# Attention by half batches, a first run fixed to expert 0, independent scatters and three transpose banks in an attention and mixture-of-experts kernel

## The chip, the cores and the metric

The kernel runs on one core of one Trainium2 chip. The metric is the device time of one execution in microseconds; the median of the runs is what counts. Beside it there is a profile of one execution, which shows every engine's instructions in time. The engines are TensorE (PE; its weight loads are shown as PEld), VectorE (DVE), ScalarE (ACT), GpSimd (POOL) and SyncE (SP, which here only issues DMAs). Each engine works through its own queue in order; an instruction that waits holds up everything behind it on that engine.

## What is computed

The inputs are x (4 x 1024 x 1024), a context (4 x 1024 x 256), the weights of a key projection and of eight experts, all float32.

```
kv   = ctx @ W_k.T + b_k
p    = layernorm(x)
out  = p @ kv                              # 1024 x 256 for each batch
sim  = (out @ kv.T) / 32
attn = softmax(layernorm(sim) * ln_gamma + ln_beta)
x1   = x + attn

h      = layernorm(x1)                      # 4096 tokens
probs  = softmax(h @ gate_w); the best two experts of each token, weights normed
y(tok) = sum over its two experts e of weight * ((silu(h @ w1[e]) * (h @ w3[e])) @ w2[e])
result = x1 + y
```

## The kernel before

The program has two stages, one after the other.

**Attention and routing.** Work is cut into 4 batches of 8 blocks of 128 tokens (G is 8, HG is 4 blocks, a half batch). `front(b)` is a list of 13 steps that a batch needs before its blocks can be finished: `context` (load and transpose the context), `values` (kv, and its bias on DVE), `keys` (transposed kv, centred), and for each of two halves four times `first_norm` (load a block of x, normalize it into `pn`, transpose it into `pT`) and once `attend` (32 matmuls' records into `pm_o`, copied to `oT`). `back(b, g)` finishes one block: four matmuls into `sim` (L323), the sum of squares on ACT (L330), a power on POOL (L198 and L200), `z` on DVE (L332), the row minimum (L334), the exponential on ACT (L338), `x1` on DVE (L342), its layernorm to `hn` (L206 to L210), the transposes of `hn` on PE (L217) with copies on ACT, the gate matmuls `pm_g` (L351) and a copy of the logits, `lg` (L360). `sim`, `z`, `x1`, `hn`, `pn` and the transposes each have two buffers. `route` takes the logits of several blocks, picks experts, and computes the slot of each token; `put` scatters the token ids to `id_d` (L450) from POOL.

The order of emission is: all of `front(0)`, then for each batch its eight `back` blocks, with the 13 steps of `front(b + 1)` spread between them; batch 3 has none to spread. A scheduler then sets the order on each engine, starting from this emission. After the last `route`, DVE computes a small table: the number of runs (`run_n`, L544), and for each run its expert, its kind and its first slot (`run_e`, `run_k`, `run_s`, L546 to L567).

**Experts.** Before the loop `load_rows` loads the ids of the first run's tokens (L686), clamps them on DVE (`rd`, L694), and gathers five groups of rows of h with POOL's indirect DMAs (L697). `load_first` loads the first tiles of w1 and w3. Both take the expert and the slot from the table through registers of SP. `tokens_in` transposes the rows: ten groups of four transposes into `pt_h` (L737), each copied by ACT or DVE (L742, L746), all through one bank of PSUM (the pool `pst`, one buffer).

The loop runs `run_n` times, eight in the profiled execution. Each run handles up to two token blocks of one expert, and all its PE work is in an order written by hand, with matmuls L838 for w1 and w3, and L894 for w2. At the end of a token block `tokens_out` transposes the output (`pt_y`, L783), adds it with the token's weight to the rows (L785), and scatters the rows to the result by an indirect DMA on POOL (L790). The last quarter of a run's last block is left for the next run, and after the loop for `leftover`, with the same bank and the same scatters. Scatters all write the result, and each waits for the one before.

Of the kernel before, what the change touches and what calls it, by code (L numbers as in the profile page):

```python
# [9 lines left out]
F32 = mybir.dt.float32  # L10
I32 = mybir.dt.int32
AF = mybir.ActivationFunctionType
ALU = mybir.AluOpType
# [6 lines left out]
P = 128  # L20
N = 512
# [4 lines left out]
MOST = HOLD[-1]  # L26
# [3 lines left out]
TOP_K = 2  # L30
# [4 lines left out]
def kernel(  # L35
# [14 lines left out]
    nc = tc.nc  # L50
# [8 lines left out]
    NT = T // P  # L59
    KM = M // P  # L60
    MAXQ = -(-T // MOST)
    NRUN = (T * TOP_K + E * (MOST - 1)) // MOST
    TAB = 16
    REG = T + -(-(MOST + P) // P) * P
    NONE = 2 * T
# [34 lines left out]
    with ExitStack() as st:  # L100
# [39 lines left out]
        def clear_slots():  # L140
            for r in range(0, E * REG, ID_R):
                n = min(ID_R, E * REG - r)
                step = nc.sync.dma_start(
                    out=id_d[r : r + n, :].rearrange("(p r) w -> p (r w)", p=P),
                    in_=none[:, : n // P * IDW],
                )
                tc.keep_in_program_order(step)
                cleared.append(step)
# [321 lines left out]
        base = None  # L470
        puts, to_put = [], []
        ready = []
        for i, step in enumerate(front(0)):
            step()
            if i == 3:
                later_loads()
        for b in range(B):
            todo = list(front(b + 1)) if b + 1 < B else []
            n_steps = len(todo)
            for g in range(G):  # L480
                back(b, g)
                for _ in range(min(len(to_put), TOP_K)):
                    to_put.pop(0)()
                while todo and (n_steps - len(todo)) * G < n_steps * (g + 1):
                    todo.pop(0)()
                if b == 0 and g == 0:
                    clear_slots()
                t = b * G + g
                if ready and t >= ready[0][1]:
                    u = ready.pop(0)[0]  # L490
                    base = route(u, lgs.pop(u), base)
                for u, (t0, m) in enumerate(GROUPS):
                    if t == t0 + m - 1:
                        ready.append((u, t + (1 if u >= len(GROUPS) - 3 else RG // 2)))
        for u, _ in ready:
            base = route(u, lgs.pop(u), base)
        for step in to_put:
# [5 lines left out]
        def row(name, n=E):  # L503
            return tb.tile([1, n], F32, name=name)
# [17 lines left out]
        for j in range(MAXQ):  # L522
            nc.vector.scalar_tensor_tensor(
                nr, n_e, float(j * MOST), nr, ALU.is_gt, ALU.add
            )
        kind, hold = row("kind"), row("hold")
        nc.vector.memset(kind, 0.0)
        nc.vector.memset(hold, float(HOLD[0]))
# [47 lines left out]
    with ExitStack() as st:  # L576
# [97 lines left out]
        def expert(i):  # L674
            return nc.values_load(
                run_e[:, ds(i, 1)], engines=(ENG.SP,), min_val=0, max_val=E - 1
            )

        def first_slot(i):
            return nc.values_load(  # L680
                run_s[:, ds(i, 1)], engines=(ENG.SP,), min_val=0, max_val=(E - 1) * REG + T
            )
# [11 lines left out]
            nc.vector.tensor_scalar(rd, ids[:, :, 0], T - 1, None, ALU.min)  # L694

        def gather(dst, src, rd, s, n):
            nc.gpsimd.indirect_dma_start(  # L697
                out=dst,
                out_offset=None,
                in_=src,  # L700
                in_offset=bass.IndirectOffsetOnAxis(ap=rd[:n, s : s + 1], axis=0),
            )
# [17 lines left out]
        def load_rows(s0):  # L720
            load_ids(ids0, s0)
            where_from(rd0, ids0)
            for s, r in enumerate(ROWS):
                gather(rows[s][:r, :], h_d, rd0, s, r)

        def load_first(i, j):

            weights(wts_in[j], (w1f, w3f)[j], expert(i), 0, KD, 0)

        def tokens_in(then=None):  # L730


            def step(s, h):
                r = ROWS[s]
                pt = pst.tile([P, 4, P], F32, tag="pt", name="pt_h")
                for k in range(HK):
                    nc.tensor.transpose(  # L737
                        pt[:, k, :r], rows[s][:r, ts(HK * h + k, P)], ident[:r, :r]
                    )
                dst = x[:, ds(HK * h, HK), ds(s * P, r)]  # L740
                if h % 2:
                    nc.vector.tensor_copy(dst, pt[:, :, :r])  # L742
                    if then is not None:
                        then(s)
                else:
                    nc.scalar.copy(dst, pt[:, :, :r])  # L746

            return [lambda s=s, h=h: step(s, h) for s in range(RT) for h in range(2)]
# [24 lines left out]
                p5=v[:, T1, :], p6=t2, p7=t[:, 1, :],  # L773
            )

        def tokens_out(ids, split, q, y):

            yv = y.rearrange("p (d c) -> p d c", d=2)

            def step(s, r):  # L780
                pt = pst.tile([P, 4, P], F32, tag="pt", name="pt_y")
                for d in range(2):
                    nc.tensor.transpose(pt[:r, d, :], yv[:, d, ds(s * P, r)], ident)  # L783
                part = rows[s][:r, ts(q, QW)]
                nc.vector.scalar_tensor_tensor(  # L785
                    part, pt[:r, 0:2, :].rearrange("p a b -> p (a b)"),
                    ids.bitcast(F32)[:r, s, 1:2], part, ALU.mult, ALU.add,
                )
                if q == DQ - 1:
                    nc.gpsimd.indirect_dma_start(  # L790
                        out=of,
                        out_offset=bass.IndirectOffsetOnAxis(ap=ids[:r, s, 0:1], axis=0),
                        in_=rows[s][:r, :],
                        in_offset=None,
                        bounds_check=T - 1,
                        oob_is_err=False,
                    )

            return [lambda s=s, r=r: step(s, r) for s, r in enumerate(split)]

        def leftover():
            return tokens_out(ids1, ROWS, DQ - 1, y1)

        def run(i, ex, s0, blocks, width):
            n = width // 2
# [10 lines left out]
            def take_ids():  # L816
# [3 lines left out]
                nc.vector.tensor_copy(rd, rd0)  # L820
                return ids, rd

            late = leftover()
            right = token_factors(n)
            for b in range(blocks):
# [41 lines left out]

                def rows_of_out(s):
                    if s < len(split):
                        gather(rows[s][: split[s], :], of, rd, s, split[s])  # L870

                late += tokens_in(rows_of_out)
                if not last:
# [1 line left out]
                for q in range(DQ):  # L875
                    pp = banks()
                    i2 = 0
                    for u, kn in enumerate(W2K):
                        j = load(w2f, 2 * i2, kn, q * QW)
                        left = weight_sums(j, kn, True)  # L880
                        todo = [
                            (p, k) for k in range(kn // 2) for p in ORDER
                        ] if u < len(W2K) - 1 else [
                            (p, k) for p in ORDER for k in range(kn // 2)
                        ]
                        if last and q == DQ - 1 and u == len(W2K) - 1:

                            assert j % WR == WR - 1 == 2
                            load_first(i + 1, 0)
                            load_first(i + 1, 1)  # L890
                            late.append(lambda: weight_sums(0, KD, False))
                        hid = [hidden_factors(g[:, i2 + k, :, :], n) for k in range(kn // 2)]
                        for at_m, (p, k) in enumerate(todo):
                            nc.tensor.matmul(  # L894
                                pp[p][:, :n], left[p][:, k, :], hid[k][p],
                                start=(i2 + k == 0), stop=(i2 + k == NI - 1),
                            )
                            if late and at_m % 7 == 6 and i2 + at_m // 7 > 0:
                                late.pop(0)()
                        i2 += kn // 2  # L900
                    if last and q == DQ - 1:
                        combine(pp, n, y1, XW)
                        break
                    y = gp.tile([P, 2 * XW], F32, tag="y", name="y", bufs=1)
                    combine(pp, n, y, XW)
                    late += tokens_out(ids, split, q, y)
            assert not late

        load_rows(first_slot(0))
        load_first(0, 0)  # L910
        load_first(0, 1)
        for step in tokens_in():
            step()
        weight_sums(0, KD, False)
        n_run = nc.values_load(run_n, min_val=1, max_val=NRUN)
        with tc.For_i(0, n_run) as i:  # L916
# [3 lines left out]
            for k in tc.Switch(kind, len(RUNS)):  # L920
                with tc.manual_schedule(engines={ENG.PE}):
                    run(i, ex, s0, *RUNS[k])
        for step in leftover():
            step()


# [26 lines left out]
```

## Time and profile before

| | before |
|---|---|
| median of 3 runs | 8942.93 us (8942.44 to 8948.6) |
| the profiled execution | 8943.72 us, span 8941.9 us |
| PE busy | 8736.7 us, 98% of the span |
| DVE busy | 4822.9 us, 54% |
| ACT busy | 666.7 us, 7% |
| POOL busy | 446.1 us, 5% |
| first loop matmul starts | 545.94 us |
| loop, to the last matmul's result | about 546 to 8918 us |

The span is the time from the first to the last instruction in the profile; the execution's own time lies 1.8 us above it. Busy times are sums over the whole span. The granted clock is the share of TensorE's full clock that it was given in a stretch. Rows of the timeline begin with the start and the duration in microseconds, then engine, line, operation, and tiles; in brackets stands the idle time of the engine before it, and what ended it. A row with a count (x8) is several instructions of the kind merged. A float32 matmul of the program shows as two records.

### The profile page before, as it was taken

To read this page: it belongs to the slowest core of one execution; us is meant where nothing else is said; L and a number is where in the kernel's file an instruction comes from. 1 tells how busy PE (TensorE), PEld (TensorE's weight loads), DVE (VectorE), ACT (ScalarE), POOL (GpSimd) and SP (SyncE) were. 2 spreads that over 40 slices of the span, in tenths; PEclk is the share of its full clock that TensorE was granted. 3 is DMA by queue.
4 is the path that set the end of the run, shared out by engine and by line. 5 is a ranking of instruction groups with operands and counts; after the bars stand their busy time and mean duration, and the time that the engine had idled before them with its cause. 6 is when DMAs were issued, how large, how long until landed. Compare 5 with 4: busy or idle time off the path is not lost. (4 is left out here: it accounts for less than half of the span.)

```text
span 8941.9 us, 99381 instructions
## 1 busy us (share of the span) xinstructions
PE 8736.7 (98%) x40738; PEld 7530.9 (84%) x40739; DVE 4822.9 (54%) x8820; ACT 666.7 (7%) x1170; POOL 446.1 (5%) x512
## 2 busy tenths in 40 slices
PE   8979999999999999999999999999999999999999
PEld 5569998999988888888888888888888888888887
DVE  5654645555554545546455554556555464555545
ACT  3310000000000000000000000000000000000000
POOL 2310000000000000000000000000000000000000
PEclk9979999999999999999999999999999999999999
DMA  3232332323232232323333232233323233232322
GB/s 140 110 101 88 105 105 91 110 93 112 96 104 83 91 103 89 103 91 102 101 95 101 92 108 84 95 103 94 110 93 103 86 103 96 90 102 91 105 87 93
DMA packets 769237, 882.16 MB, mean 99 GB/s; under 512 B 33424, under 2 KB 729232, under 8 KB 768608
## 3 DMA queue, kind: packets, MB, share of 16 engines
q1 hardware_dynamic: 734096, 766.12, 26.5%
q0 software_dynamic: 34368, 107.84, 3.6%
q8 instruction: 357, 5.85, 0.3%
q14 instruction: 272, 2.23, 0.1%
q10 hardware_dynamic: 144, 0.13, 0.0%
HBM read 803.61 MB, written 74.87 MB: 98 GB/s over the span
## 5 line engine op out<-in xcount | busy, mean ns | idle before, releaser
L838 PE MATMUL ps<-x,w 128*128 128x262 f32 (+5 forms) x10752 | 2489.2, 381 | 78.9 <-issue 77.8
L838 PEld LDWEIGHTS ps<-x,w 128*128 128x128 f32 x10752 | 2043.9, 191 | 370.3 <-issue 80.6
L838 PE MATMUL ps<-xs,s 128*128 128x262 f32 (+5 forms) x7168 | 1625.9, 379 | 0.0
L838 PEld LDWEIGHTS ps<-xs,s 128*128 128x128 f32 x7168 | 1355.0, 189 | 195.1
L633 DVE TENSOR_TENSOR s<-w 128x512 f32<-128x512 f32 (+2 forms) x769 | 479.6, 624 | 1638.1 <-DMA w<-in_L_ffn_w_dram 1634.4
L894 PE MATMUL ps<-g,s 128*128 128x262 f32 (+5 forms) x3584 | 1026.1, 379 | 0.0
L894 PE MATMUL ps<-t,w 128*128 128x262 f32 (+5 forms) x3584 | 1024.9, 379 | 0.0
L894 PE MATMUL ps<-g,w 128*128 128x262 f32 (+5 forms) x3584 | 904.6, 381 | 0.0
L838 PE MATMUL ps<-xs,w 128*128 128x262 f32 (+5 forms) x3584 | 848.2, 379 | 0.0
L838 PE MATMUL ps<-x,s 128*128 128x262 f32 (+5 forms) x3584 | 848.2, 380 | 0.0
L672 DVE TENSOR_TENSOR c<-ps,vu 128x524 f32<-128x524 f32 (+5 forms) x448 | 309.8, 691 | 919.7 <-PE ps L838 919.7
L894 PEld LDWEIGHTS ps<-g,s 128*128 128x128 f32 x3584 | 680.1, 190 | 95.3 <-DVE y L672 0.4
L838 PEld LDWEIGHTS ps<-x,s 128*128 128x128 f32 x3584 | 680.9, 190 | 94.1
L838 PEld LDWEIGHTS ps<-xs,w 128*128 128x128 f32 x3584 | 678.6, 189 | 96.4
L894 PEld LDWEIGHTS ps<-t,w 128*128 128x128 f32 x3584 | 678.8, 189 | 96.1
L766 DVE TENSOR_TENSOR t<-g 128x262 f32<-128x262 f32 (+5 forms) x896 | 375.5, 424 | 677.1 <-PE ps L894 674.0
L894 PEld LDWEIGHTS ps<-g,w 128*128 128x128 f32 x3584 | 651.4, 190 | 76.6
L767 DVE TENSOR_TENSOR t<-g,t 128x524 f32<-128x524 f32 (+5 forms) x896 | 613.1, 689 | 16.5
L663 ACT COPY p1s<-ps 128x262 f32<-128x262 f32 (+5 forms) x512 | 191.1, 373 | 4623.5 <-PE ps L838 2432.9
L894 PE MATMUL ps<-t,s 128*128 128x262 f32 (+5 forms) x1792 | 512.9, 380 | 0.0
L634 DVE TENSOR_TENSOR s<-s,w 128x512 f32<-128x512 f32 (+2 forms) x769 | 475.9, 619 | 10.1
L635 DVE TENSOR_TENSOR s<-w,s 128x512 f32<-128x512 f32 (+2 forms) x769 | 474.4, 617 | 0.0
(170 smaller groups left out, 4863.8 us busy)
## 6 DMA issues: line engine op xcount, KB each, us to landing
w<-in_L_ffn_w_dram SPq DMA_DIRECT2D x450, 1024.0 KB, 5.1
w<-in_L_ffn_w_dram SPq DMA_DIRECT2D x256, 768.0 KB, 4.5
w<-in_L_ffn_w_dram SPq DMA_DIRECT2D x64, 512.0 KB, 3.5
xt<-in_x_dram SPq DMA_DIRECT2D x32, 512.0 KB, 4.3
out_dram<-x SPq DMA_DIRECT2D x32, 512.0 KB, 2.9
h_d<-hn SPq DMA_DIRECT2D x32, 512.0 KB, 2.6
cx<-in_ctx_dram SPq DMA_DIRECT2D x4, 1024.0 KB, 5.5
id_d<-none SPq DMA_DIRECT2D x5, 512.0 KB, 10.7
```

The lines of the kernel that those rows point to most:

```text
L633: nc.vector.tensor_tensor(f["p5"], a21, a22, ALU.add)
L634: nc.vector.tensor_tensor(f["p6"], f["p5"], a11, ALU.subtract)
L635: nc.vector.tensor_tensor(f["p3"], a12, f["p6"], ALU.subtract)
L663: nc.scalar.copy(p1s, one[:, :n])
L672: nc.vector.tensor_tensor(mid, qc[:, :, :n], vu, ALU.add)
L766: nc.vector.tensor_tensor(t2, v[:, B22, :], v[:, T1, :], ALU.subtract)
L767: nc.vector.tensor_tensor(t[:, 1:3, :], v[:, B11 : B21 + 1 : B21 - B11, :], t2.unsqueeze(1).to_broadcast([P, 2, n]), ALU.subtract,)
L838: nc.tensor.matmul(pp[p][:, :n], left[p][:, k, :], right[p][:, k, :], start=(k == 0), stop=(k == HK - 1),)
L894: nc.tensor.matmul(pp[p][:, :n], left[p][:, k, :], hid[k][p], start=(i2 + k == 0), stop=(i2 + k == NI - 1),)
```

## The change

The list of `front` steps of each batch is cut in two: `context` (of the next batch) goes to the half before, then `values`, `keys`, four norms and the first attend are a half, and four norms and the second attend are another. Only the first half of batch 0 is emitted ahead of the blocks. Then, for each four blocks, the steps of the next half are spread between them. So the last four blocks of all have no steps between them, where before it was the last eight.

Expert 0 is given one run at least (`nr` of expert 0 is at least 1), so that the first run is always expert 0's and its first slot is 0: the loads before the loop use constants. The number of runs that the table may hold is computed to match (it is 15 either way).

The scatters of one token block are declared independent of each other. The gathers of result rows are made to wait for the scatters that were sent since the run began. Outside the loop the transposes use the three double banks of the matmuls (`ps2`), not the single one.

```diff
-    NRUN = (T * TOP_K + E * (MOST - 1)) // MOST
+    NRUN = (T * TOP_K + E * MOST - (E - 1)) // MOST
...
-        for i, step in enumerate(front(0)):
+        halves = []
+        for b in range(B):
+            steps = list(front(b))
+            cut = 3 + HG + 1
+            halves.append(steps[1:cut])
+            halves.append(steps[cut:])
+            if b == 0:
+                first_steps = [steps[0]] + halves.pop(0)
+            else:
+                halves[-3].append(steps[0])
+        for i, step in enumerate(first_steps):
             step()
             if i == 3:
                 later_loads()
-        for b in range(B):
-            todo = list(front(b + 1)) if b + 1 < B else []
-            n_steps = len(todo)
-            for g in range(G):
-                back(b, g)
...
-                while todo and (n_steps - len(todo)) * G < n_steps * (g + 1):
-                    todo.pop(0)()
...
+        for t in range(NT):
+            if t % HG == 0:
+                todo = halves.pop(0) if halves else []
+                n_steps = len(todo)
+            back(*divmod(t, G))
+            for _ in range(min(len(to_put), TOP_K)):
+                to_put.pop(0)()
+            while todo and (n_steps - len(todo)) * HG < n_steps * (t % HG + 1):
+                todo.pop(0)()
...
+        nc.vector.tensor_scalar(nr[:, 0:1], nr[:, 0:1], 1.0, None, ALU.max)
...
         def gather(dst, src, rd, s, n):
-            nc.gpsimd.indirect_dma_start(
+            return nc.gpsimd.indirect_dma_start(
...
-        def load_first(i, j):
+        def load_first(ex, j):
 
-            weights(wts_in[j], (w1f, w3f)[j], expert(i), 0, KD, 0)
+            weights(wts_in[j], (w1f, w3f)[j], ex, 0, KD, 0)
...
+        def bank(spare, name):
+
+            if spare:
+                t = ps2.tile([P, 2, N], F32, tag="ps2", name=name)[:, 0, :]
+                return t.rearrange("p (a b) -> p a b", b=P)
+            return pst.tile([P, 4, P], F32, tag="pt", name=name)
...
-        def tokens_out(ids, split, q, y):
+        sent, blocks_sent = [], []
+
+        def tokens_out(ids, split, q, y, spare=False):
 
             yv = y.rearrange("p (d c) -> p d c", d=2)
+            blocks_sent.append(0)
+            group = f"rows{len(blocks_sent)}"
 
             def step(s, r):
-                pt = pst.tile([P, 4, P], F32, tag="pt", name="pt_y")
+                pt = bank(spare, "pt_y")
...
                 if q == DQ - 1:
-                    nc.gpsimd.indirect_dma_start(
+                    put = nc.gpsimd.indirect_dma_start(
...
+                    if s:
+                        tc.declare_no_dep(put.ins, group=group, reason="rows are different")
+                    tc.add_to_no_dep_group(group, put.ins)
+                    sent.append(put)
...
-                        gather(rows[s][: split[s], :], of, rd, s, split[s])
+                        got = gather(rows[s][: split[s], :], of, rd, s, split[s])
+                        for put in sent:
+                            tc.add_manual_dep(got.ins, put.ins.name, SYNC)
+                    if s == RT - 1:
+                        sent.clear()
...
-        load_rows(first_slot(0))
+        load_rows(0)
         load_first(0, 0)
         load_first(0, 1)
-        for step in tokens_in():
+        for step in tokens_in(spare=True):
             step()
...
-        for step in leftover():
+        for step in leftover(spare=True):
             step()
```

More of the change, by code (lines that the diff above doesn't have):

```diff
@@ L476 @@
                 later_loads()
-        for b in range(B):
-            todo = list(front(b + 1)) if b + 1 < B else []
-            n_steps = len(todo)
-            for g in range(G):
-                back(b, g)
-                for _ in range(min(len(to_put), TOP_K)):
-                    to_put.pop(0)()
-                while todo and (n_steps - len(todo)) * G < n_steps * (g + 1):
-                    todo.pop(0)()
[L486 to L494, printed above, removed]
+        for t in range(NT):
[7 more added lines that the diff above has]
+                todo.pop(0)()
+            if t == 0:
+                clear_slots()
+            if ready and t >= ready[0][1]:
+                u = ready.pop(0)[0]
+                base = route(u, lgs.pop(u), base)
+            for u, (t0, m) in enumerate(GROUPS):
+                if t == t0 + m - 1:
+                    ready.append((u, t + (1 if u >= len(GROUPS) - 3 else RG // 2)))
         for u, _ in ready:
@@ L724, in load_rows, with tokens_in @@
                 gather(rows[s][:r, :], h_d, rd0, s, r)
-        def load_first(i, j):
-            weights(wts_in[j], (w1f, w3f)[j], expert(i), 0, KD, 0)
-        def tokens_in(then=None):
+        def load_first(ex, j):
[5 more added lines that the diff above has]
+            return pst.tile([P, 4, P], F32, tag="pt", name=name)
+        def tokens_in(then=None, spare=False):
             def step(s, h):
                 r = ROWS[s]
-                pt = pst.tile([P, 4, P], F32, tag="pt", name="pt_h")
+                pt = bank(spare, "pt_h")
                 for k in range(HK):
@@ L797, in step, with leftover @@
                     )
+                    if s:
+                        tc.declare_no_dep(put.ins, group=group, reason="rows are different")
+                    tc.add_to_no_dep_group(group, put.ins)
+                    sent.append(put)
             return [lambda s=s, r=r: step(s, r) for s, r in enumerate(split)]
-        def leftover():
-            return tokens_out(ids1, ROWS, DQ - 1, y1)
+        def leftover(spare=False):
+            return tokens_out(ids1, ROWS, DQ - 1, y1, spare)
         def run(i, ex, s0, blocks, width):
@@ L869, in rows_of_out @@
                     if s < len(split):
-                        gather(rows[s][: split[s], :], of, rd, s, split[s])
+                        got = gather(rows[s][: split[s], :], of, rd, s, split[s])
+                        for put in sent:
+                            tc.add_manual_dep(got.ins, put.ins.name, SYNC)
+                    if s == RT - 1:
+                        sent.clear()
                 late += tokens_in(rows_of_out)
@@ L888, in run @@
                             assert j % WR == WR - 1 == 2
-                            load_first(i + 1, 0)
-                            load_first(i + 1, 1)
+                            load_first(expert(i + 1), 0)
+                            load_first(expert(i + 1), 1)
                             late.append(lambda: weight_sums(0, KD, False))
```

## The prediction

> **What bounds the kernel now.** I read the page's busy shares, then the stretches, the timeline around the edited places, and the chain of waits. TensorE is busy 98% of the span, but this mean hides three stages. The stretches view (us, then busy us and instruction count of PE, PEld, DVE, ACT, POOL, then granted clock, DMA share, GB/s):
>
> ```profile
> 380.00:400.00 20.00, 20.00 (x92) 12.34 (x91) 9.45 (x33) 7.36 (x14) 11.08 (x14) 1.00 0.16 57
> 460.00:480.00 20.00, 11.59 (x52) 10.89 (x52) 12.34 (x46) 3.80 (x7) 3.97 (x6) 0.54 0.29 119
> 500.00:520.00 20.00, 0.00 (x0) 0.00 (x0) 11.91 (x103) 0.00 (x0) 6.95 (x8) 0.50 0.32 97
> ...
> 546.00:8918.00 8372.00, 8298.05 (x38856) 7249.82 (x38856) 4491.84 (x7868) 489.94 (x832) 269.10 (x228) 1.00 0.30 97
> 8918.00:8942.00 24.00, 3.14 (x10) 1.25 (x10) 2.85 (x6) 0.00 (x0) 4.89 (x5) 0.54 0.22 89
> ```
>
> The expert loop (546 to 8918) is full at full clock; nothing of its TensorE work is edited, so the change can only move the 546 us before it and the 24 us after it. In the attention (to 498) TensorE is full while two batches mix, and half empty at half clock once batch 3 runs alone, from 403 to 498. From 498 to 546 it waits for the route table, ids, rows and transposes.
>
> The timeline shows how long four blocks take when their chain starts from empty:
>
> ```profile
> 80.54 12.50 PE L323 MATMUL sim<-kvT,oT 128*128 128x512 f32 x28
> 84.56 1.28 DVE L332 SCALAR_TENSOR_TENSOR z<-sim,r,ngam 128x1024 f32<-128x1024 f32 x1 [3.40 <-POOL r L200]
> 95.81 0.81 DVE L210 TENSOR_SCALAR hn<-x,mv,r 128x1024 f32<-128x1024 f32 x1 [1.35 <-POOL r L200]
> 104.93 0.81 DVE L210 TENSOR_SCALAR hn<-x,mv,r 128x1024 f32<-128x1024 f32 x1 [0.71 <-POOL r L200]
> 117.91 0.81 DVE L210 TENSOR_SCALAR hn<-x,mv,r 128x1024 f32<-128x1024 f32 x1 [0.71 <-POOL r L200]
> 129.37 0.81 DVE L210 TENSOR_SCALAR hn<-x,mv,r 128x1024 f32<-128x1024 f32 x1 [1.62 <-POOL r L200]
> ```
>
> First z 4.0 us after the first sim; the four hn at 11.3, 20.4, 33.4 and 44.8 us after that z. The lone batch 3 repeats it: first z at 407.58, third and fourth hn at 443.10 and 452.92, 35.5 and 45.3 after. The stage before the loop and the end:
>
> ```profile
> 512.39 0.42 SPq L686 DMA_DIRECT2D ids<-id_d  x1
> 515.62 0.99 POOL L697 DMA_INDIRECT rows<-h_d,rd  x1 [11.22 <-DVE rd L694]
> 524.09 1.09 PE L737 MATMUL pt_h<-ident,rows 128*128 128x128 f32 x4 [26.09 <-DMA w<-in_L_ffn_w_dram]
> 540.73 0.42 DVE L742 COPY x<-pt_h 128x256 f32<-128x256 f32 x1 [1.93 <-PE pt_h L737]
> ...
> 8920.66 1.03 POOL L790 DMA_INDIRECT out_dram<-rows,ids  x1 [144.41 <-DVE rows L785]
> 8924.83 0.99 POOL L790 DMA_INDIRECT out_dram<-rows,ids  x1 [3.14 <-DVE rows L785]
> 8928.93 0.97 POOL L790 DMA_INDIRECT out_dram<-rows,ids  x1 [3.12 <-DMA out_dram<-rows,ids]
> 8933.04 0.97 POOL L790 DMA_INDIRECT out_dram<-rows,ids  x1 [3.13 <-DMA out_dram<-rows,ids]
> 8937.13 0.92 POOL L790 DMA_INDIRECT out_dram<-rows,ids  x1 [3.12 <-DMA out_dram<-rows,ids]
> ```
>
> Four of the last five scatters are 4.1 us apart: each waits for the landing of the one before.
>
> **End: scatters independent, three banks.** A POOL issue with nothing to wait for takes 1.26 us (the gathers at 515.62, 516.92, 518.18). So the fifth goes out at 8920.66 + 4 x 1.26 = 8925.7, not 8937.13: 11.4 us. The rows keep pace: with one bank they come each 1.27 us, with three sooner. The 2.14 MB at the 410 GB/s of one scatter need 5.2 us, about the issue time; I allow 0.5 us for them meeting. Gain 10.9 (8 to 11.5). Inside the loop the same freedom is worth nothing: POOL is idle there, 3168 us in the waits view for rows alone. The added waits of the out gathers on the scatters stand in POOL's queue with only gathers behind, whose rows are first used after the first output quarter, 44 us later; were that cover gone, one scatter's 3.3 us per run of eight would show.
>
> **Before the loop.** The ids load waited for run_s (cast at 511.06); now it waits for the last put alone, which landed at 505.7 (where DVE's memset of ids1 is released), so it goes at about 506.1. In the changed instruction order SP still reads run_n (cast at 502.13) first, so the weights follow the ids and do not start earlier than that; DVE's rd moves ahead of some 35 small ops, which then end at about 512, and run_k by 516, before the loop reads it. Ids, both 1 MB weight loads and five gathers keep their mutual order: all shift by 6.2. The ten transposes alternate with their copies on one bank, 524.09 to 541.15 = 17.1 us; on three banks TensorE goes on, 8 x 1.11 + 2 x 0.69 at half clock + the last copy 0.7 = 11.0. Gain 6.1; rows landing at more than 2.2 us apart would eat it (bound 0). The added max is one DVE op, 0.15. Together 12.2 (6 to 13).
>
> **Attention by halves.** The first half's front and first attend are in the same order: it ends at 46.9 as now. Then come seven windows with front work and four blocks without. In the changed order the sixteen sim matmuls of a window's four blocks stand behind the attend that makes their oT, and on DVE every op of a window's four blocks (last lg, route) stands ahead of the next window's first z. So DVE, ACT and POOL have almost nothing to do in the attend (13.8 us), and each window starts the chain from empty; before, back lagged a whole batch, and sims of other blocks stood on both sides of each attend.
> A window with norms only (four): oT copy 0.75 + sim to z 4.0 + third hn 34.4 (mean of 33.4 and 35.5) + 0.8 + its transposes, gate and last pn transposes 4.3 + attend 13.8 = 58. The first has no route: 55. The last has the fourth hn ahead of its attend, without later blocks between: 61 to 68, taken 62.
> A window with context, values and keys (three): hn of the block before 0.9, sim 0.4, gate 1.7, context transposes and sim rest 3.6, then Square and r: z at 9.2; fourth hn 45 later + 0.8; transposes and gate 3.4; attend 13.8: 72. The stretch measured from 80.54 lacked the eight kv adds (0.42 each) but had more bn_stats; I take 71.
> The last four blocks: first z at 4.7, last lg after 43.8 (448.99 to 492.80) to 51.4 (407.58 to 458.93): 54 in all.
> Sum: 46.9 + 55 + 58 + 58 + 62 + 3 x 71 + 54 = 547, where the last lg is now at 492.8: 54 us lost. If the faster cadence of 228 to 245 (an hn every 8.5 us or so) held in each window: 53, 65.5, 57, 46 instead: 46.9 + 3 x 53 + 3 x 65.5 + 57 + 46 = 505, 13 lost. If DVE stalls at lg another 3 us a window: 75 lost. xt and cx loads move with their steps on SP; they were issued tens of us ahead and stay so (SP waits there only for x and hn).
>
> A rule that bears on it: after the 6.66 us gap at 222, ten sim records took 6.54 us against 4.3, and after the 3.65 us gap at 96.7 the clock read 0.83 and 0.77 for two stretches of 20 us, some 8 us lost. [...] Each new window has such a gap before its first hn (sims done at about 10, hn at 16). [...]
>
> **Sum.** 54 - 12.2 - 10.9 = +31; I shade it to +29, towards the faster cadence. The profiled run took 8943.7 (span 8941.9, 1.8 outside), 0.8 above the median of 8942.9. Forecast 8972.
>
> **Rivals.**
> [...]
> Faster: the halves mix as well as whole batches do, some 109 us per eight blocks (attends ending at 151.9, 262.1 and 371.3). Then 46.9 + 28 x 13.6 + 49 = 477, 16 gained, 8904 in all. It decides if a window averages under 56.7 us; mine average 64. Against it speaks the DVE order.
> Worse: lg waits in DVE's queue hold each window 3 us more: 8993.
> Not as said: the scatters stay chained by something else: 11 us more on any case.
>
> **Chances.** A measurement of this kernel tells about 0.2%, 18 us. Forecast's case, with the worse one, 0.66, nearly all above 8961; small change 0.21; as good a mix 0.13. Slower 0.65, same 0.22, faster 0.13. The range goes from the small change's low side, 8934, to 9006, the worse case and the chained scatters with it.
>
> **What would show it.** Right: the attends some 58 and 71 us apart in turn; TensorE empty for 5 us or more before the first hn of each window, the clock under 1.0 up to 500; last lg at about 545; first ids load 13 us after it (now 19.6); the pt_h row 11 us long; loop of 8372 us; five scatters 1.3 us apart. Wrong: attends under 57 us apart, or a loop of another length.

## The result, and the profile after

The changed kernel takes 9011.81 us (median of four runs, 9008.7 to 9012.53) against 8944.72 for the kernel before on the same chip (8942.44 to 8948.6): ratio 1.0073, 95% interval 1.0059 to 1.0086. It is slower, as forecast, but by 67 us where 29 was forecast, and outside the range (9006). The profiled execution has a span of 9009.8 us, 67.9 above that of before.

First the stretches of the changed kernel (us, then busy us and instruction count of PE, PEld, DVE, ACT, POOL, then granted clock, DMA share, GB/s):

```profile
220.00:240.00 20.00, 12.81 (x47) 9.47 (x47) 13.70 (x37) 4.18 (x7) 11.16 (x14) 0.58 0.45 161
240.00:260.00 20.00, 20.00 (x77) 11.11 (x76) 5.90 (x31) 5.55 (x11) 3.08 (x9) 1.00 0.13 43
580.00:600.00 20.00, 7.01 (x32) 6.87 (x32) 13.60 (x132) 1.39 (x3) 7.81 (x8) 0.50 0.09 30
624.90:8999.00 8374.10, 8297.97 (x38863) 7250.37 (x38864) 4494.85 (x7870) 490.76 (x832) 269.60 (x228) 1.00 0.30 97
8999.00:9010.00 11.00, 0.98 (x4) 0.43 (x4) 1.50 (x4) 0.00 (x0) 4.88 (x5) 0.50 0.49 194
```

The loop is what it was: 8374.2 us from its first matmul to the first of the last scatters, 8374.7 before. So the time went where only the attention runs. There TensorE is no longer full while two batches mix (the stretch at 380 in the profile before): stretches at a clock of 0.58 and two thirds busy (220 to 240) take turns with full ones (240 to 260, half of it the attend, most of the rest the next sims). DVE has the reverse: 13.7 us of work in the first, 5.9 in the second.

The timeline of TensorE in one window with norms only, from the end of an attend to the next attend (start, us, engine, line, operation, tiles; in brackets the idle time before it and what ended it):

```profile
186.76 14.31 PE L324 MATMUL sim<-kvT,oT 128*128 128x512 f32 x32
204.72 1.10 PE L218 MATMUL pt<-ident,hn 128*128 128x128 f32 x8 [3.65 <-DVE hn L211]
206.06 1.88 PE L352 MATMUL pm_g<-gw,hT 128*128 128x8 f32 x8 [0.24 <-ACT hT L219]
...
219.00 1.09 PE L218 MATMUL pt<-ident,pn 128*128 128x128 f32 x4
...
227.98 1.94 PE L218 MATMUL pt<-ident,hn 128*128 128x128 f32 x8 [7.19 <-DVE pos L449]
229.79 1.88 PE L352 MATMUL pm_g<-gw,hT 128*128 128x8 f32 x8
...
234.89 14.92 PE L299 MATMUL pm_o<-pT,kv 128*128 128x512 f32 x32
```

Two gaps, one before the first hn and a longer one before the third, and after each TensorE's work takes twice as long, behind the first gap from the gate records on: eight transposes 1.94 us where the first eight took 1.10, eight gate records 1.88 where the same take 0.95 ahead of the last attend (518.37). The same in a window with context, values and keys, here from its last hn on:

```profile
306.26 1.94 PE L218 MATMUL pt<-ident,hn 128*128 128x128 f32 x8 [5.57 <-DVE mv L209]
308.07 1.88 PE L352 MATMUL pm_g<-gw,hT 128*128 128x8 f32 x8
309.80 2.06 PE L299 MATMUL pm_o<-pT,kv 128*128 128x512 f32 x2
311.65 1.71 PE L352 MATMUL pm_g<-gw,hT 128*128 128x8 f32 x8
313.22 15.84 PE L299 MATMUL pm_o<-pT,kv 128*128 128x512 f32 x30
```

Two records of the attend take 2.06 us, where 32 take 14.0 in the very first (32.84): the attend starts at half clock too, and lasts from 309.80 to 329.06. The hn it waited for was itself late, in VectorE's timeline and then in POOL's:

```profile
305.24 0.87 DVE L211 TENSOR_SCALAR hn<-x,mv,r 128x1024 f32<-128x1024 f32 x1 [2.84 <-POOL r L201]
```

```profile
300.94 0.78 POOL L199 TENSOR_SCALAR v<-mv 128x1 f32<-128x1 f32 x1 [9.98 <-DVE pos L449]
302.01 1.33 POOL L451 DMA_INDIRECT id_d<-tok,pos  x1 [0.28 <-DVE pn L211]
303.64 0.96 POOL L451 DMA_INDIRECT id_d<-tok,pos  x1 [0.30 <-issue]
304.62 0.58 POOL L201 TENSOR_TENSOR r<-v,nhalf 128x1 f32<-128x1 f32 x1
```

Between `v` and the `r` made from it, POOL issues two id scatters.

The attends end at 46.8, 108.3, 186.9, 249.8, 329.1, 389.6, 469.0 and 532.3 us, so the seven windows last 61.5, 78.6, 62.9, 79.3, 60.6, 79.3 and 63.3 us (forecast 55, 71, 58, 71, 58, 71, 62). The last lg comes at 586.5, where it came at 492.8: 93.7 lost, 54 forecast. The stages behind it, in the timelines of SP, TensorE and POOL:

```profile
599.60 0.39 SPq L698 DMA_DIRECT2D ids<-id_d  x1
```

```profile
610.53 5.31 PE L756 MATMUL pt_h<-ident,rows 128*128 128x128 f32 x24 [18.82 <-DMA rows<-h_d,rd]
616.14 1.77 PE L756 MATMUL pt_h<-ident,rows 128*128 128x128 f32 x16 [0.30 <-DMA rows<-h_d,rd]
624.94 5.72 PE L868 MATMUL ps<-x,w 128*128 128x246 f32 x16 [7.03 <-issue]
```

```profile
8999.10 1.02 POOL L813 DMA_INDIRECT out_dram<-rows,ids  x1 [144.41 <-DVE rows L808]
9000.42 0.99 POOL L813 DMA_INDIRECT out_dram<-rows,ids  x1 [0.31 <-DVE rows L808]
...
9004.27 0.93 POOL L813 DMA_INDIRECT out_dram<-rows,ids  x1 [0.30 <-issue]
```

From the last lg to the loop's first matmul it is now 38.4 us, before 53.1: 14.7 gained. From the first of the last scatters to the end it is 10.7, before 21.2: 10.5 gained. With 0.5 from the loop, 93.7 - 14.7 - 10.5 - 0.5 = 68.0, the difference of the spans.

### The profile page after: what moved, and what is told of

Same layout as the page of the kernel before. It is cut to its first block, busy times and chain, and to the rows that moved or that the text cites. A ratio compares the mean times of both kernels' runs of the same rounds, so it can differ in the third digit from the quotient of the medians.

```text
span 9009.8 us, 99390 instructions
## 1 busy us (share of the span) xinstructions
PE 8784.3 (97%) x40738; PEld 7571.1 (84%) x40739; DVE 4829.8 (54%) x8821; ACT 673.1 (7%) x1170; POOL 441.7 (5%) x512
## 6 DMA issues: line engine op xcount, KB each, us to landing
id_d<-none SPq DMA_DIRECT2D x5, 512.0 KB, 10.7
```

## The experiments

The runs in one table: the last lg from each one's profile, the medians, and the ratios against the kernel before on the same chip. The two runs without id scatters leave the table of slots mostly empty, so their experts work on other rows: only their attention, up to the last lg, is compared.

| run | last lg, us | median, us | ratio and interval |
|---|---|---|---|
| halves only | 586.9 | 9034.98 | 1.0101 (1.0086 to 1.0116) |
| all but the halves | 493.9 | 8919.07 | 0.9971 (0.9961 to 0.9982) |
| independent scatters only | 492.7 | 8935.64 | 0.9987 (0.9981 to 0.9994) |
| first run only | 493.9 | 8938.64 | 0.9991 (0.9983 to 0.9999) |
| banks only | 497.0 | 8937.17 | 0.9989 (0.9982 to 0.9996) |
| extra matmuls in the gaps | 573.5 | 8995.53 | 1.0059 (1.0044 to 1.0075) |
| the same, last window's moved | 565.1 | 8998.07 | 1.0063 (1.0048 to 1.0079) |
| no id scatters | 571.5 | 8999.51 | 1.0063 (1.0046 to 1.0079) |
| moved extra matmuls, no id scatters | 552.5 | 8980.74 | 1.0045 (1.0030 to 1.0060) |
| attend two blocks early | 511.2 | 8937.41 | 0.9992 (0.9983 to 1.0000) |
| attend three blocks early | 516.9 | 8942.94 | 0.9996 (0.9987 to 1.0004) |
| even, lead 1 | 548.6 | 8972.35 | 1.0031 (1.0019 to 1.0043) |
| even, lead 2 | 492.0 | 8915.88 | 0.9970 (0.9959 to 0.9980) |
| even, lead 3 | 469.8 | 8894.95 | 0.9945 (0.9931 to 0.9958) |
| even, lead 4 | 475.2 | 8900.22 | 0.9950 (0.9936 to 0.9964) |

### The parts alone

**Halves only.** The loop over half batches in the kernel before, nothing else.

```
+        for t in range(NT):
+            if t % HG == 0:
+                todo = halves.pop(0) if halves else []
+                n_steps = len(todo)
+            back(*divmod(t, G))
...
+            while todo and (n_steps - len(todo)) * HG < n_steps * (t % HG + 1):
+                todo.pop(0)()
```

> The kernel before with nothing but the attention by half batches taken over. Theory (the whole loss is the longer attention, the other parts add to it without interaction): last lg at about 586 as in the changed kernel, loop entry and end as before, so 94 us over the kernel before: 9038 (9033 to 9043). Rival (the other parts cost something hidden, or only pay in this company): under 9025 or over 9050.

90 us over the kernel before (8944.75 on this chip), near the 94 expected, with the last lg at 586.9. The long attention is the halves' own doing.

**All but the halves.** The changed kernel with the loop of before (`for b in range(B)`, `front(b + 1)` spread over eight blocks).

> The changed kernel with the attention loop of the kernel before put back; first run is the first expert's, independent scatters and three banks stay. Theory: last lg at 493 as before, about 14 us gained ahead of the loop and 10.5 at the end, so 8919 (8916 to 8923), faster than both kernels by 25 and 93 us. Rival (part of the gain ahead of the loop comes only with the halves): 8925 to 8932.

8919.07, 25.7 us under the kernel before. From last lg to the first loop matmul it is 38.2 us. The two runs together, 90.2 - 25.7 = 64.5, are the changed kernel's 67.1 within the medians' wander: no sign that the parts act on each other.

**One part at a time.** Independent scatters alone, with the waits of the gathers:

```
+                    if s:
+                        tc.declare_no_dep(put.ins, group=group, reason="rows are different")
+                    tc.add_to_no_dep_group(group, put.ins)
+                    sent.append(put)
...
+                        for put in sent:
+                            tc.add_manual_dep(got.ins, put.ins.name, SYNC)
```

> The kernel before with only the scatters of a block made independent (and the output gathers made to wait for them). By the traces of the two kernels the end should be 10.5 us shorter, nothing else moves: 8934 (8932 to 8936). Rival (the added waits of the gathers cost in the loop, repaid by something else in the changed kernel): 8938 or more.

11.3 us under the kernel before (8946.9 on this chip); in its profile the end takes 10.8 us instead of 21.2. The added waits cost nothing that shows.

The first run fixed to expert 0:

```
+        nc.vector.tensor_scalar(nr[:, 0:1], nr[:, 0:1], 1.0, None, ALU.max)
...
-        load_rows(first_slot(0))
+        load_rows(0)
```

> The kernel before with only the first run taken as the first expert's, so that its ids and weights wait for no table of runs. On record: 6.2 us less ahead of the loop, so 8938.5 (8936 to 8941). Rival (the rows land earlier, but the single bank or the loop's own table then ends last): 8942 or more. Second rival (more than forecast, because of the 14 to 15 us seen ahead of the loop where 12 were forecast): 8936 or less.

8.3 us under the kernel before; from the last lg (493.9) to the loop (540.20) it is 46.3 us, 6.8 less than before.

The banks:

```
-                pt = pst.tile([P, 4, P], F32, tag="pt", name="pt_h")
+                pt = bank(spare, "pt_h")
```

> The kernel before with only the three banks for transposes outside the loop. On record: 6.1 us less ahead of the loop, and nothing at the end while its scatters are chained (each waits for the landing of the one before): 8938.6 (8936 to 8941). Rival (the five gathers of rows land so far apart that the transposes wait for them, not for the bank): 8942 or more.

9.7 us under the kernel before. The profiled execution is the slowest of its 21, with an attention 4 us longer, which the edit does not touch; so only what follows its last lg (497.0) is read: to the loop it is 44.9 us, 8.2 less. The two rows of its TensorE timeline that decide:

```profile
527.92 4.30 PE L744 MATMUL pt_h<-ident,rows 128*128 128x128 f32 x24 [25.78 <-DMA rows<-h_d,rd]
541.87 6.56 PE L845 MATMUL ps<-x,w 128*128 128x246 f32 x16 [5.97 <-issue]
```

24 transposes in 4.30 us are 0.18 each; on one bank four took 1.09 to 1.12, 0.28 each. The granted clock there was 0.50 throughout (530 to 546 in the kernel before); on three banks the next eight, at 533.58, took 1.06 us, the time of eight hn transposes at full clock. The forty transposes take 6.0 us, where 10.3 had been counted, and waits for rows (1.36 and 0.58) take part of that back. So this part was worth 2 us more than the 6.1 on record. 6.8 + 8.2 is 15.0, what both together gave (14.9).

### Why the windows are long: clock and POOL's queue

**Extra matmuls in the gaps.** Eight 128x512 matmuls on data that is there already, whose product nobody reads, ahead of the hn transposes in each window's gap; TensorE's order is otherwise kept.

```
+            ahead = HG - 2 if h == 0 and b < B - 1 else HG - 1
+            if i == ahead and (b, h) != (B - 1, 1):
+                warm = ps_t.tile([P, 4, P], F32, tag="pt", name="warm")
+                for k in range(8):
+                    nc.tensor.matmul(
+                        warm.rearrange("p a b -> p (a b)"), oT[:, 0, ts(i, P)], oT[:, 1, :],
+                        start=True, stop=True,
+                    )
```

> The changed kernel with eight extra 128x512 matmuls on an already loaded oT ahead of the hn transposes that precede each window's attend (7 windows), in TensorE's gap there; their product is read by nobody, all else keeps its order. Theory (the missing time is TensorE at half clock in the gate, the pn transposes and the start of the attend): windows with norms only shorter by about 3 us, those with context, values and keys by about 5, 25 in all: 8987 (8980 to 8995). Rival (DVE and POOL set the windows): 9008 or more, since the extra matmuls then only delay hn.

More work on TensorE, and 16 us less time. In its timeline, a window with norms only, then one with context:

```profile
213.46 7.11 PE L352 MATMUL warm<-oT 128*128 128x512 f32 x16
220.81 1.06 PE L218 MATMUL pt<-ident,hn 128*128 128x128 f32 x8 [0.24 <-DVE pos L457]
222.17 1.06 PE L360 MATMUL pm_g<-gw,hT 128*128 128x8 f32 x8 [0.29 <-ACT hT L219]
...
300.56 1.10 PE L299 MATMUL pm_o<-pT,kv 128*128 128x512 f32 x2
301.50 0.96 PE L360 MATMUL pm_g<-gw,hT 128*128 128x8 f32 x8
302.31 13.12 PE L299 MATMUL pm_o<-pT,kv 128*128 128x512 f32 x30
```

What took 1.94, 1.88, 2.06, 1.71 and 15.84 takes 1.06, 1.06, 1.10, 0.96 and 13.12. Six windows are 1.3 to 4.7 us shorter, 22 in all. But the seventh is 8 longer: its gap lies ahead of the third block's hn, and I had put the matmuls ahead of the fourth's, where they held up work that was ready. So they were moved:

```
-            ahead = HG - 2 if h == 0 and b < B - 1 else HG - 1
+            ahead = HG - 2 if h == 0 else HG - 1
```

> The run with eight extra matmuls in each window's gap, with those of the seventh window moved to its third block, where its gap of 7.2 us is. Theory (clock): the seventh window gains 4 us where it lost 8, so last lg 573.5 - 12 = 561 (559 to 564), 8984. Rival (the extra matmuls of that window delay hn wherever they stand): last lg 570 or later.

Last lg at 565.1; the first six windows are now 25 us shorter than in the changed kernel, as the clock theory had it (their order is that of the run above, which won 22: so much do two profiles differ). The seventh is 4 us longer still, so for that window the expectation failed. VectorE's and TensorE's timelines of this run:

```profile
488.27 0.87 DVE L211 TENSOR_SCALAR hn<-x,mv,r 128x1024 f32<-128x1024 f32 x1 [2.09 <-POOL r L201]
```

```profile
484.55 0.64 PE L218 MATMUL pt<-ident,pn 128*128 128x128 f32 x4
...
485.84 1.05 PE L218 MATMUL pt<-ident,pn 128*128 128x128 f32 x4
489.28 1.94 PE L218 MATMUL pt<-ident,hn 128*128 128x128 f32 x8 [2.39 <-DVE hn L211]
491.10 1.88 PE L360 MATMUL pm_g<-gw,hT 128*128 128x8 f32 x8
```

The fourth hn waits for a power that stands behind four id scatters in POOL's queue (482.50 to 487.63). But it does so in the changed kernel too, and comes 38.9 us after the window's first z in both. What is longer is the attend: 18.2 us for 14.9, its first two records 2.05 for 1.10 and the other thirty 14.76 for 13.12. The extra matmuls end at 482.04, and TensorE is slow again from about 486: the four transposes at 485.84 take 1.05 us where four took 0.64 at 484.55, ahead of the 2.39 us for which TensorE then waits for hn. In the changed kernel the cold stretch lay earlier, and the clock was full again just before the attend (0.66 from 516 to 517, 1.00 from 517 to 518). The four runs of this kernel spread from 8988 to 9008, the profiled one being the quickest; only the profile is used here.

**No id scatters.** All but those of the last two blocks left out.

```
                 lambda t=t, k=k: put(t, k) for t in range(t0, t0 + m) for k in range(TOP_K)
+                if t >= NT - 2
```

> The changed kernel without the id scatters (left out for all tokens but the last two blocks of 128; the table of slots then stays empty there, the counts, runs and all TensorE work are the same); TensorE's and VectorE's order in the attention is unchanged. Read at the last lg, not at the end, since the loop's gathers and scatters meet other rows. Theory that POOL's queue has a part (the trace shows the last hn of a context window waiting 2.8 us for a r that stands behind two id scatters): that hn comes 2.5 to 3 us earlier in three windows, and its gap ahead of the attend, 5.6 us, shrinks to about 3, so part of the half clock goes too: last lg 8 to 20 us earlier, 567 to 578. Rival (those waits only lengthen what the clock or the hn chain takes anyway): last lg within 4 us of 586.5. Total, if nothing but the attention moves: 8992 to 9012.

Last lg 15 us earlier: the three context windows are 3.5 to 4.3 shorter, those with norms only unchanged within 0.2, the last four blocks 3.4 shorter. VectorE and TensorE at the same place as above:

```profile
297.75 0.81 DVE L211 TENSOR_SCALAR hn<-x,mv,r 128x1024 f32<-128x1024 f32 x1 [0.72 <-POOL r L201]
```

```profile
298.71 1.07 PE L218 MATMUL pt<-ident,hn 128*128 128x128 f32 x8 [2.67 <-DVE hn L211]
300.07 1.61 PE L352 MATMUL pm_g<-gw,hT 128*128 128x8 f32 x8 [0.29 <-ACT hT L219]
301.54 2.05 PE L299 MATMUL pm_o<-pT,kv 128*128 128x512 f32 x2
303.38 1.71 PE L352 MATMUL pm_g<-gw,hT 128*128 128x8 f32 x8
304.95 15.94 PE L299 MATMUL pm_o<-pT,kv 128*128 128x512 f32 x30
```

The wait for r falls from 2.84 to 0.72 and TensorE's gap from 5.57 to 2.67, but the attend is as cold as ever. So I had one half of this wrong: the shorter gap did not save the clock. The gain is the queue's alone.

**Both.** The moved matmuls and no id scatters.

> The same without the id scatters of all but the last two blocks of 128 (left out; the slots then stay empty there). Theory (clock and POOL's queue are two separate causes): their gains add, 25 and 15 us, last lg at 546 to 550, which is the forecast's 547 without a route's scatters. Rival (they overlap: both shorten the same gap): 555 to 562, and something else is missing in the account.

552.5, between the two expectations. The seventh window now is 2.4 shorter than in the changed kernel, and 6.4 shorter than with the moved matmuls alone: without the scatters its fourth hn comes 35.3 us after the first z, not 38.9, TensorE has no gap there, and the slow stretch, which begins at 483 in this run too (four transposes at 482.86 take 1.03 us), is over ahead of the attend (its first two records, at 486.80, take 1.10). The context windows stay at 75 us: hn is there at 288.60 in one of them, but its transposes begin at 292.88, when the extra matmuls are done. The extra matmuls cost there what the queue would have given. Together the two causes are worth 34 us (586.5 - 552.5) of the 93.7 that the attention lost, at least; extra matmuls that fit the gap were not tried. The other 60 are near the 54 that the forecast gave to chains that start from empty; the next runs bear on those.

### What the order should have been

**The attend earlier.** The next half's front steps are paced so that its attend is emitted after the second of four blocks; in a second run (HG - 3 for HG - 2) after the first.

```
-            while todo and (n_steps - len(todo)) * HG < n_steps * (t % HG + 1):
+            while todo and (n_steps - len(todo)) * (HG - 2) < n_steps * (t % HG + 1):
```

> The changed kernel, but a window's front steps are paced so that its attend is emitted after the window's second block, not after its fourth: two blocks' vector work then stands beside the attend. Theory (windows are long because the chain starts from empty and TensorE is cold for it): windows between the whole-batch cadence (54.5 us for four blocks) and 62 instead of 69 on average, last lg at 490 to 540, 8920 to 8960 in all, granted clock higher in the windows. Rival (a window's length is set by the hn chain of its own four blocks and POOL's scatters of ids, wherever the attend stands): within 10 us of the changed kernel, 9000 or more.

Last lg at 511.2, 75 us earlier, 8937.41. Windows average 57.7 us; the attend runs at full clock (32 records take 13.90 to 14.00 us at 198.75, 264.51 and 318.47).

> The changed kernel with the front of the next half batch paced one step further than in the run before: its attend is emitted after the window's first block, so that three blocks' vector work stands beside it. The run with two blocks beside it had its last lg at 511 us, the whole-batch order at 493. Theory (an attend costs nothing when other blocks' chains stand beside it, and the price of a lead is only a longer start): last lg at 490 to 505, 8916 to 8932. Rival (a lead of two is already enough, the third only delays the first blocks and stalls on the front's own steps): last lg at 511 or later, 8937 to 8950.

516.9: the rival was right, a third block beside the attend brought nothing when the front steps stay bunched in one block.

**Spread evenly, with a lead.** The front steps of a half are spread over four blocks, which end one to four blocks before the half is needed.

```
-            if t % HG == 0:
+            if t % HG == 3 or t == 0:     # lead 1; 2 and 1 for leads of 2 and 3
                 todo = halves.pop(0) if halves else []
-                n_steps = len(todo)
+                n_steps, since = len(todo), t
+                until = t + (HG if t else 3)
...
-            while todo and (n_steps - len(todo)) * HG < n_steps * (t % HG + 1):
+            while todo and (n_steps - len(todo)) * (until - since) < n_steps * (t - since + 1):
```

> The same with a lead of one block. Theory: with one block beside each attend there is part of a chain from empty in each window, so some 5 us a window over the whole-batch cadence; half 1's attend at about 105, 24 blocks of 15, five blocks' drain of 58: last lg at about 523 (500 to 530), 8925 to 8955. Rival (evenness alone is enough, the lead is nothing): last lg at 490, 8915.

> The changed kernel with the half batches' front steps spread evenly over four blocks, each attend emitted two blocks ahead of the first block that needs it (the first half's front, then half 1 within blocks 0 and 1, then evenly). Theory (windows are long because a window's work bunches: front steps first, then a chain from empty; spread evenly, the halves run at the whole-batch cadence of 13.6 us a block): 93 us to half 1's attend, 24 blocks of 13.6, then six blocks' drain of 60 to 70: last lg at 480 to 490, 8905 to 8916. Rival (the lead alone decides, evenness is nothing): as the bunched lead of two, last lg at 511, 8937.

> The same with a lead of three blocks. Theory: half 1's attend at about 80 us, 24 blocks of 13.6, then seven blocks' drain of about 80: last lg at about 486 (480 to 493), 8905 to 8919. Rival (lead alone): as the bunched lead of three, 517, 8943.

With one block of lead the last lg is at 548.6, beyond the theory's range, which ended at 530: its windows still last 53 to 72 us. With two it is 492.0, 2 us past the range, where the bunched order with the same lead had 511. With three it is 469.8, better than expected: windows of 51 us on average, under the whole-batch order's 54.9, and a drain of 65.8 where that has 89. The lg groups of the changed kernel and of this one (duration ns min/median/max, first and last start):

```profile
L361 DVE COPY lg<-pm_g x32: 153/167/168, 70.2 to 586.5; 128x8 f32<-128x8 f32 x32
```

```profile
L361 DVE COPY lg<-pm_g x32: 146/167/168, 70.3 to 469.8; 128x8 f32<-128x8 f32 x32
```

And the same hundred microseconds in both, first the changed kernel, then the even lead of three (columns as above):

```profile
200.00:300.00 100.00, 83.45 (x367) 60.44 (x365) 59.80 (x144) 35.77 (x68) 25.16 (x42) 0.80 0.36 128
```

```profile
200.00:300.00 100.00, 93.48 (x438) 59.62 (x437) 72.25 (x192) 40.23 (x78) 39.98 (x63) 0.97 0.35 126
```

The clock is 0.97, not 0.80, and DVE does a fifth more work in the same time.

A lead of four puts both halves of batch 0 ahead of the first block (`first_steps += halves.pop(0)`).

> Half batches spread evenly with a lead of four: both halves of the first batch ahead of block 0. Theory (the mix is full from a lead of three on; a longer lead only lengthens the start and the drain by a block): last lg at 475 to 490, 8900 to 8915, slower than a lead of three. Rival (a longer lead still improves the mix): last lg under 470, under 8895.

475.2 and 8900.22: slower than a lead of three by its longer drain, 80 us against 66, though its seven windows are 9 us shorter in all. The best kernel here is the even lead of three, 8894.95 us, 50 us under the kernel before and 117 under the changed one. It has all the other parts of the change, and its blocks start as early as in the changed kernel.

## Why the prediction was right in its sign and wrong in its size

**Right.** The change loses in the attention and gains before the loop and at the end. Windows alternate between short and long, TensorE is empty before the first hn (for 3.64 to 3.74 us, where 5 had been named), the last four blocks take 54.2 us (54 forecast), the ids load goes out 13.1 us after the last lg (13 forecast), the five scatters are 1.3 us apart, the loop keeps its length. The end brought 10.5 (10.9 forecast), the stage before the loop 14.7 (12.2), the difference being mostly the banks, whose transposes had been counted at half clock.

**Wrong.** The term that failed is the seven windows: 55 + 58 + 58 + 62 + 3 x 71 was 446, measured 485.5. What failed is the step "its transposes, gate and last pn transposes 4.3 + attend 13.8" and "transposes and gate 3.4; attend 13.8": full-clock durations, put behind a gap. From the start of the hn that an attend waits for to the attend's end, the forecast had 18.9 us (0.8 + 4.3 + 13.8) in a window with norms only and 18.0 (0.8 + 3.4 + 13.8) in one with context. Measured in the first six windows, it is 24.4, 22.8 and 23.0 in the former and 22.6, 23.8 and 23.9 in the latter: 29.6 us more in the six together. The prediction had weighed the clock at a window's first gap, where other work hides part of it, and not at the gap ahead of the attend, where nothing does. With the moved extra matmuls the same stretches take 19.7, 18.9 and 18.9, the forecast's own figure, and 19.2 to 19.4. So the clock is shown by experiment for 25 of the 30 us in that profile.

The other terms are small. The first z of a window came 0.8 to 0.9 us later after the attend than forecast, in all seven: 6 us. Taking 71 instead of 72.2 cost 3.6, and the 3 us taken off the first window for want of a route did not show. The chain of hn was sized well, or a little long: in the windows at 108.3, 249.8 and 389.6 the fourth came 46.1, 45.4 and 45.5 us after the first z (forecast 45), in those at 46.8, 186.9 and 329.1 the third came after 31.5, 34.4 and 31.9 (forecast 34.4), 3.4 less in all. 29.6 + 6 + 3.6 + 3 - 3.4 is 38.8 of the 39.5. The id scatters' 15 us are no part of this difference, as the hn came near their forecast times although the scatters stood in POOL's queue. They are a cost in the changed kernel that the forecast did not see as one; what they cost the kernel before was not run.

The shade "towards the faster cadence" from 31 to 29 went the wrong way as well. The prediction's own rows, ten sim records in 6.54 us against 4.3 behind a gap, pointed the other way. After the gap of 3.65 us ahead of 204.72 the clock read 0.50 from 206.5 till past 220, under steady work. One reading of the profile was too broad, though no term rests on it: batch 3 alone was not at half clock from 403 on, as the clock of the kernel before read 1.00 from 400 to 420 and 0.74 from 420 to 440.

**The rivals.** The one called worse (VectorE's waits for lg, 3 us a window, 8993) was nearest in time, but not in cause: such waits would have made the hn late, and the hn came within 1.1 us of their forecast or early. The faster mix was wrong by its own test, windows of 69 us on average where it needed 56.7; yet it is what the halves give when their steps are spread evenly, 51 us a window with a lead of three. That the scatters stay chained is ruled out, and so is the small change, the low end of the range: it had the attention 13 us longer, and it was 93.7.

## What to carry to other kernels

To cut a pipeline's lead shortens its start and its drain, but the lead is also what stands beside the long matmuls: count in blocks how much other work each queue has while the longest step runs, and spread the steps evenly before you shorten the lead. Put no full-clock duration behind a gap in TensorE: look for the gap on the path, and take the rows that follow a gap (here eight hn transposes took 1.94 us behind a gap of 7.19, and 1.06 where extra matmuls filled it). On an in-order queue, a short scalar step that others wait for (here a power on POOL) should not stand behind a batch of DMA issues (without the id scatters hn waited 0.72 us for it, with them 2.84).

## What the runs showed of the hardware

The half clock after a gap did not have one length. In the changed kernel the same order of transposes and 8-column gate matmuls stands behind a gap of 3.65 us in three windows. In one (204.72) the half clock lasted from 206 till past 220, where the next gap begins; in the two others it ended after some 9 us of work (346.86 to 356, 486.76 to 496). With 128x512 matmuls right behind a gap of 6.38 us, in the even lead of three, six records took 4.39 us. At full clock two take 1.02 there and four 1.88, so six some 2.74; by that some 3.3 us were cold:

```profile
266.90 4.39 PE L324 MATMUL sim<-kvT,oT 128*128 128x512 f32 x6 [6.38 <-DVE z L333]
271.13 1.04 PE L218 MATMUL pt<-ident,hn 128*128 128x128 f32 x8
```

But the thirty records at 313.22 of the changed kernel, 128x512 too, took 15.84 us for 13.12 at full clock, so some 5.4 us of them were cold, after 7 us of other cold work. The kind of work may matter; no run varied it alone.

Nor did a gap stand right ahead of every slow stretch. In the run with the moved matmuls the rows turned slow at about 486 (485.84), 4 us after the extra matmuls had ended, with no gap over 0.3 us since. In the run with extra matmuls first, the last thirty records of the last attend (504.02) took 14.82 us for 13.12, and the longest gap in the 19 us ahead of it was 0.29. And without id scatters a gap of 2.67 us was followed by transposes that were still fast (1.07); the slow rows began 1.4 us later. What sets the moment is left open by these runs.
